# Moving the sums of the ffn's weight product, and writing out GpSimd's order around sixteen gathers, in a fused attention and ffn block

## The chip, the cores and the metric

One Trainium2 chip, one of its cores. The time is that of the device in microseconds. TensorE is called PE here, VectorE DVE, ScalarE ACT, GpSimd POOL and SyncE SP; SP only issues DMAs. PE's weight loads are listed apart as PEld.

## The reference

32 sequences of 64 tokens, 1024 wide, all in float32. A layer with a low-rank adapter per sequence, grouped-query attention with rotary embedding, then two layers with routed low-rank experts, two residuals:

```python
def cond(x, label):          # adapter chosen by the sequence's label
    low = einsum('bsi,bir->bsr', x, lora_A[label])
    return x @ W.T + einsum('bsr,or->bso', low, lora_B) * 0.5
def attn(x):                 # 32 heads of 32, 8 kv heads, causal
    q, k, v = split(x @ w_qkv.T + b_qkv)
    p = softmax(mask(rope(q) @ rope(k).T / sqrt(32)))
    return (p @ v) @ w_o.T + b_o
def cond2(x, language):      # top 2 of 8 experts of rank 16, biased by language
    gates = top2_softmax(x @ Wr.T + 5 * onehot(language))
    return x @ W2.T + 2 * einsum('bter,bte,eor->bto', x @ A, gates, B)
def ffn(x):                  # the same form, own router, with a bias
    return x @ W_base.T + b_base + 2 * experts(x)
x = x + attn(cond(x, label))
x = x + ffn(cond2(x, language))
```

## The kernel before

Two neighbouring linear layers are multiplied together first: cond's weights with w_qkv ("cq" and "ckv"), and cond2's with the ffn's base weights ("cf", with the identity added for the residual). Then two halves of 16 sequences (`hf` = 0, 1) run one after the other: projection to q and k (`qk_pair`, column groups 4, 0, 1, 2, 3), v, attention in eight units, the output projection, and the ffn.

Every large product follows one scheme: a 2 x 2 block product with seven block multiplications instead of eight (`Group`). Its steps p1, p6, p5, p7, p2, p3, p4 are each one block multiplication into the PSUM banks x, y and z; the sums of weight blocks (s1 to s4) are made on POOL (`weight_sums`, L179 to L182), those of column blocks (t1 to t4) on DVE (`column_sums`, L191 to L197). p1's result is copied by ACT (L282), p6's and p7's are added to it by DVE (`u1`, L288, and `u2`, L300), and `out` finishes a block (outputs of cq, ckv and cf: L580, L582).

**The product cf** (168 to 296 us) has four groups g = 0 to 3. Its blocks stay in SBUF, in the tile `cf`, which groups 0 and 1 fill (kappa = 0) and groups 2 and 3 fill again (kappa = 1). The ffn uses the scheme twice, one inside the other, so for each kappa seven sets of eight factors are needed: `level_one` (L741) adds whole blocks, two tiles of 128x512, `level_two` (L753 to L756) adds quarters of them and issues four DMAs of 256 KB into the scratch `cf7` (L758). All these sums are on DVE. `levels(kappa)` lists the eleven steps. The list of kappa 0 is worked off behind the steps of group 2, that of kappa 1 after the last group and after the two `low_rows` of b2f (L515). The steps also hold `narrow` (cx, a narrow product per group) and `wo_sums` (sums of w_o's blocks, one at a time: load by SP, four sums on POOL, DMA out by POOL).

Temporary tiles come from one ring of eleven, `tp`, through `tmp`: a twelfth request waits until the first tile has been read for the last time, by a DMA too. The weights `w` and the sums `s` come from rings of two.

**The ffn** runs the seven products n = 0 to 6, which are p1, p6, p2, p7, p5, p3 and p4 of the outer scheme (`SEVEN`), each in two quarters q = 0, 1; a `Quarter` is itself a group of seven blocks, 128x256 each. `begin` does p1 and p6, then the quarter before is finished (p4, p3), then `middle` does p5, p2, p7 and out11. Outer products that must be added to each other are kept in four accumulators a, b, c, z of SBUF; `known` (L1410) adds an accumulator to p1's, p6's or p7's sum on POOL, and `out_f` (L1419, L1426) adds that to the bank on DVE. `c` has the tag of `a`.

**The gathers.** The adapter's rows of each sequence are fetched by an indirect DMA, issued by POOL (L440). Those of the first half go into tiles of the pool `gen`; those of the second half into the unused half of its tile `q`, and are issued in two runs of eight, after the last POOL sum of n = 2 and of n = 3 (`late["gather0"]`, `late["gather1"]`).

**Order.** Where `tc.manual_schedule` stands, the engines named keep the order in which the code records their instructions; elsewhere a scheduler orders them by its own estimates, and it also merges what is recorded inside and outside such a block. Up to the first half's beginning SP, PE and DVE are in written order, POOL and ACT are not; in the ffn only PE is.

Of the kernel before, what the change touches and what calls it, by code (L numbers as in the profile page):

```python
# [19 lines left out]
P = 128  # L20
# [56 lines left out]
def block_kernel(ctx: ExitStack, tc: tile.TileContext, a, out: bass.AP):  # L77
# [354 lines left out]

    def gathered(hf, s, new, n):

        tiles = []
        for b0 in range(0, BS, n):
            t = new(f"a1_{hf}_{s}_{b0}")
            for b in range(n):
                at = hf * BH + s * BS + b0 + b
                nc.gpsimd.indirect_dma_start(  # L440
                    t[:, b, :],
                    None,
                    a["a1"],
                    bass.IndirectOffsetOnAxis(ap=rows_of[:, at : at + 1], axis=0),
                )
            tiles.append(t)
        return tiles
# [59 lines left out]
    with tc.tile_pool(name="gen", bufs=1) as gen:  # L507

        def low_rows(name, low, right, n, dst):

            for at in range(0, n, 512):
                m = min(512, n - at)
                ps = ps_tile(f"{name}_{at}")
                for kc in range(KC):
                    nc.tensor.matmul(  # L515
                        ps[:, :m], low[:, kc, :], right[:, kc, at : at + m],
                        start=kc == 0, stop=kc == KC - 1,
                    )
                rows = tmp(f"{name}o_{at}")
                nc.scalar.copy(rows[:, :m], ps[:, :m])  # L520
                nc.scalar.dma_start(dst[:, at : at + m], rows[:, :m])
# [112 lines left out]
        def gather_first(s):  # L634
            tags = iter(("w_os", "s_os"))
            first_pass[s] = gathered(
                0, s, lambda name: gen.tile([P, 4, KC * LR], F32, tag=next(tags), name=name), 4
            )
# [95 lines left out]
        def level_one(kappa, j, x, y, op):  # L734
            if kappa == 1 and j == 1:

                wide = gen.tile([P, H, 512], F32, tag="sum0", name="cfs1")
                spare.extend(wide[:, i, :] for i in range(4))
            s = [spare.pop() if spare else tmp(f"cfs{kappa}{j}{i}") for i in range(2)]
            for i in range(2):  # L740
                op(s[i], x[i], y[i])  # L741
            sums_of_cf[j] = s

        spare = []

# [16 lines left out]

        def levels(kappa):

            s = sums_of_cf
            v = nc.vector
            one, two = partial(level_one, kappa), partial(level_two, kappa)
            b11, b12, b21, b22 = (block_of(x) for x in ("11", "12", "21", "22"))
            return [
                lambda: one(1, b21, b22, v.tensor_add),  # L770
                lambda: two("22", b22),
                lambda: two("s1", s[1]),
                lambda: one(2, s[1], b11, v.tensor_sub),
                lambda: two("s2", s[2]),
                lambda: one(3, b11, b21, v.tensor_sub),
                lambda: two("11", b11),
                lambda: one(4, b12, s[2], v.tensor_sub),
                lambda: two("12", b12),
                lambda: two("s3", s[3]),
                lambda: two("s4", s[4]),  # L780
            ]

        steps = levels(0)

        def next_steps(n, *more):
            def do(w):
                for _ in range(n):
                    steps.pop(0)()
                for step in more:
                    step(w)  # L790

            return do

        def first_w(w):
            narrow(2, w)
            first_pass["w"] = load_w(cqkv[:, :, 4 * WG : 5 * WG], "qk04")

# [8 lines left out]
                (1, "p7"): lambda w: wo_sums(4),  # L806
                (1, "p4"): lambda w: (narrow(1, w), wo_sums(5)),
                (2, "p1"): next_steps(2),
                (2, "p6"): next_steps(2, lambda w: wo_sums(6)),
                (2, "p7"): next_steps(1),  # L810
                (2, "out11"): next_steps(2),
                (2, "p2"): next_steps(2),
                (2, "p3"): next_steps(1, lambda w: wo_sums(7)),
                (2, "p4"): next_steps(1, first_w),
                (3, "p4"): lambda w: narrow(3, w),
            },
        )
        for half in range(2):
            at = slice(half * 512, (half + 1) * 512)
            low_rows(f"b2f{half}", b2, w3[:, :, at], 512, b2s[:, at])  # L820
        for step in levels(1):
            step()

# [80 lines left out]
    def scoped(name, bufs=1, side="left"):  # L904
        return pools.enter_context(tc.tile_pool(name=name, bufs=bufs, side=side, reuse_waits="tile"))

    for hf in range(2):
        x = first_pass["x"] if hf == 0 else load_x(hf)
# [4 lines left out]

        pools = ExitStack()
        qp = scoped(f"q{hf}")
        act = scoped(f"act{hf}")
        ep = scoped(f"e{hf}", 8)
        attention, pools = pools, ExitStack()
        xt = all_column_sums(f"x{hf}", scoped(f"sums_x{hf}"), x_half, 512)
        q = qp.tile([P, 2, BH, 4, S], F32, tag="q", name=f"q_{hf}")  # L920
        if hf == 0:
            low = first_pass["low"]
        else:

            low = new_low(hf)
            a1 = q[:, 1].rearrange("p b m t -> p b (m t)")
            tiles = []
            for s in range(NS):
                with tc.issue_after(late[f"gather{s}"].ins):
                    tiles += gathered(hf, s, lambda name: a1[:, s * BS : (s + 1) * BS], BS)  # L930
            steps = [ranks(hf, s, x, tiles[s : s + 1], low) for s in range(NS)]
            first_halves, second_halves, sums = zip(*steps)
# [29 lines left out]
        def qk_pair(g, z_bank=group_bank):  # L962
            w = first_pass.pop("w", None)
            if w is None:
                w = load_w(cqkv[:, :, g * WG : (g + 1) * WG], f"qk{hf}{g}")

            def out(r, c, ps, add):
                oc = 2 * g + r
                raw = tmp(f"raw_{hf}_{oc}_{c}")
                bias = bqk[:, oc : oc + 1]  # L970
                if add is None:
                    nc.scalar.activation(raw, ps, AF.Identity, bias=bias)
                else:
                    nc.vector.scalar_tensor_tensor(raw, ps, bias, add, ALU.add, ALU.add)
                rope(oc, c, raw)

            def rank(r, c, rows):
                b = b1d[rows, g, :] if (r, c) == (0, 1) else b1q[rows, (2 * g + r) * P : (2 * g + r + 1) * P]
                return b, low_half(c)[rows]

            return RankGroup(f"qk{hf}{g}", w, weight_sums(w, f"qk{hf}{g}"), xt, out, rank, z_bank)
# [310 lines left out]

# [88 lines left out]
        def accumulator(x):  # L1384
            pool, tag = {"a": (yp, "sum3"), "b": (fp, "b"), "c": (yp, "sum3"), "z": (yp, "sum2")}[x]
            acc[x] = pool.tile([P, 4, 512], F32, tag=tag, name=f"{x}_f{hf}")

        def quarter(n, q):
# [18 lines left out]
            def known(m, half, add):  # L1407
                if prior is not None:
                    to = part(prior if kept is None else kept, m, half)
                    late["sum"] = nc.gpsimd.tensor_add(to, part(prior, m, half), add)  # L1410

            def out_f(m, half, ps, add):
# [8 lines left out]
                oc = 4 * r + q + 2 * m  # L1421
                both = m in outs
                if not both:
                    outs[m] = tmp(f"o_{hf}_{oc}_{c}")
                o = outs[m][:, half * 256 : (half + 1) * 256]
# [37 lines left out]

        with tc.manual_schedule(engines={mybir.EngineType.PE}):
            rs = [logit_rows(c) for c in range(2)]
# [16 lines left out]
            for n in range(7):  # L1482
# [3 lines left out]
                if n == 4:  # L1486

                    for kc in range(H):
                        t = by_sequence(xt.whole[1][:, kc, :])
                        nc.vector.tensor_sub(t, x_half(H + kc, 0), t)  # L1490
                for q in range(2):
                    if (n, q) == (3, 0):
                        late["gather0"] = late["sum"]
                    if (n, q) == (5, 0):
                        late["gather1"] = late["sum"]
                    group = quarter(n, q)
                    group.begin()
                    if last is not None:
                        finish(last)
                    group.middle()  # L1500
                    if q == 0 and n < 6:
                        ts[n + 1] = inner_columns(n + 1)
                    last = group
                    if (n, q) == (0, 0):
                        ps = ps_tile(f"lgx_{hf}")
# [9 lines left out]
                        for c in range(2):  # L1515
                            ps = ps_tile(f"hx_{hf}_{c}")
                            nc.tensor.matmul(ps, b2f[:, D : D + P], hw[0][c], start=True, stop=True)
                            nc.vector.tensor_add(h[1, c], h[1, c], ps)
                    if (n, q) == (1, 0):
                        gs = gates_turned("3", hf, gates3)  # L1520
# [91 lines left out]
```

## Time and profile before

Three runs: median 1222.45 us (1222.40 to 1223.41). The profiled execution took 1222.28 us, its span is 1220.5 us, granted clock 0.99 in the mean.

| stretch, us | what | PE busy | DVE | POOL | granted clock |
|---|---|---|---|---|---|
| 0 to 168 | products cq, ckv | 165.0 | 48.7 | 64.2 | 1.00 |
| 168 to 296.3 | product cf, b2f | 127.5 | 56.8 | 55.7 | 1.00 |
| 296.3 to 308.3 | first step of the first half | 3.6 | 7.9 | 0.0 | 0.79 |
| 308.3 to 604 | first half to the output projection | 295.7 | 203.9 | 154.2 | 0.99 |
| 604 to 758 | first half's ffn | 149.7 | 82.9 | 52.0 | |
| 758 to 762.2 | its last quarter | 0.0 | 0.5 | 4.2 | 0.82 |
| 762.2 to 1068 | second half to the output projection | 305.8 | 207.1 | 165.7 | 0.99 |
| 1068 to 1220.5 | second half's ffn | 147.8 | 83.6 | 36.0 | 1.00 |

Busy time is the time in which an engine runs instructions. The granted clock is the share of PE's full rate that the chip allowed in the stretch; where it is below 1, the same matmuls take longer and still count as busy. The profile's list of waits names for each engine what it waited for, the total, the number and the longest; a releaser behind an arrow is the last to come. In timeline rows an idle time in brackets is the engine's idle time just before the row.

### The profile page before, as it was taken

Reading aid. Unit: us, or ns where it says so; the run is one execution under the profiler, and the core shown is the slowest. Engines: PE = TensorE matmul, PEld = TensorE weight load, DVE = VectorE, ACT = ScalarE, POOL = GpSimd, SP = SyncE. Lnnn points to the kernel's source line nnn. Section 1 sums busy time; section 2 is a strip of 40 time slices with the busy share of each in tenths; the row PEclk is TensorE's granted clock in tenths of the full one; section 3 lists DMA queues with packets and bytes.
Section 4 is the critical chain, followed back from the end, with each engine's and each line's share of the span. In section 5 each row is a group of like instructions: output and inputs, shape, how many; then the busy total and the mean of one; then the engine's idle time right before and its main releaser. Section 6 shows DMA issues by size and latency. Waiting matters only on the chain.

```text
span 1220.5 us, 15162 instructions
## 1 busy us (share of the span) xinstructions
PE 1195.1 (98%) x5916; PEld 708.7 (58%) x5916; DVE 691.4 (57%) x1221; ACT 156.7 (13%) x302; POOL 531.9 (44%) x477
## 2 busy tenths in 40 slices
PE   9999999998899999999999898999999999999998
PEld 3444874554344468544458787544458654448887
DVE  4312151455655888774757362456788864657562
ACT  1001000000000114430011000100113431011000
POOL 3441365331143656662802453334655761822231
PEclk9999999999899999999999899999999999999999
DMA  6652734675511120222216565121120122204543
GB/s 242 224 204 107 270 130 143 217 257 172 165 35 35 35 70 2 70 70 86 86 44 190 160 186 177 53 65 39 35 69 2 71 69 70 92 26 119 156 137 105
DMA packets 114679, 136.71 MB, mean 112 GB/s; under 512 B 6576, under 2 KB 92976, under 8 KB 113328
## 3 DMA queue, kind: packets, MB, share of 16 engines
q1 hardware_dynamic: 101120, 111.52, 28.7%
q10 hardware_dynamic: 10800, 15.84, 3.7%
q0 software_dynamic: 2688, 8.39, 2.0%
q8 instruction: 47, 0.77, 0.3%
q14 instruction: 24, 0.20, 0.0%
HBM read 101.02 MB, written 34.71 MB: 111 GB/s over the span
## 4 chain that ended last, share of the span: by engine, by line
PE 94%; DMA 2%; POOL 1%; DVE 1%; issue 1%; SPq 0%; ACT 0%; DVEq 0%; ACTq 0%; POOLq 0%
PE qk_y L261 9%; PE o_y L261 7%; PE qk_z L261 6%; PE qk_x L261 6%; PE f_y L261 5%; PE v L1002 5%; PE o_x L261 5%; PE o_z L261 5%; PE f_z L261 4%; PE f_x L261 4%; PE cf_y L261 3%; PE cq_y L261 3%; PE sc L1023 3%; PE pt L1076 2%; PE cq_z L261 2%; PE cf_x L261 2%
## 5 line engine op out<-in xcount | busy, mean ns | idle before, releaser
L950 POOL TENSOR_TENSOR raw<-raw,consts 128x512 f32<-128x512 f32 x40 | 63.1, 1584 | 131.4 <-DVE t L949 131.4
L1056 POOL TENSOR_TENSOR e<-e,top 128x512 f32<-128x512 f32 x64 | 64.9, 1044 | 57.3 <-DVE top L1055 42.2
L261 PE MATMUL qk_x<-x,w_qk 128*128 128x512 f32 x160 | 75.1, 612 | 8.4 <-ACT qk_p L282 8.4
L261 PE MATMUL f_y<-s_f,w_f 128*128 128x256 f32 x336 | 82.3, 380 | 0.5 <-DVE f_u L300 0.5
L1068 POOL TENSOR_TENSOR e<-e,tot 128x512 f32<-128x512 f32 x64 | 66.2, 1065 | 27.3 <-DVE tot L1066 27.3
L261 PE MATMUL qk_y<-sum_x,s_qk 128*128 128x512 f32 x160 | 72.2, 594 | 0.0
L261 PEld LDWEIGHTS f_y<-s_f,w_f 128*128 128x128 f32 x336 | 63.9, 191 | 9.7 <-DVE f_u L300 0.9
L261 PEld LDWEIGHTS qk_x<-x,w_qk 128*128 128x128 f32 x160 | 30.9, 195 | 48.3 <-issue 39.0
L261 PE MATMUL o_x<-q,w_o 128*128 128x512 f32 x128 | 58.9, 592 | 0.0
L1002 PE MATMUL v<-w_v,x 128*128 128x256 f32 x256 | 58.7, 382 | 0.0
L1177 POOL TENSOR_TENSOR x<-x,o_u 128x512 f32<-128x512 f32 x24 | 30.9, 1292 | 54.3 <-DVE o_u L1175 33.2
L1002 PEld LDWEIGHTS v<-w_v,x 128*128 128x128 f32 x256 | 47.4, 190 | 8.4 <-issue 2.7
L261 PEld LDWEIGHTS qk_y<-sum_x,s_qk 128*128 128x128 f32 x160 | 30.3, 191 | 37.6 <-issue 36.4
L951 DVE TENSOR_TENSOR t<-t,consts 128x512 f32<-128x512 f32 x40 | 48.6, 1227 | 0.7
L1065 DVE TENSOR_REDUCE tot<-e 128x8 f32<-128x512 f32 x64 | 40.5, 666 | 10.6 <-ACT e L1060 10.4
L1060 ACT ACTIVATE e<-e 128x512 f32<-128x512 f32 x64 | 38.2, 639 | 54.2 <-POOL e L1056 54.2
L1046 DVE TENSOR_TENSOR e<-sc,consts 128x512 f32<-128x512 f32 x64 | 39.7, 675 | 8.8 <-PE sc L1023 8.8
L960 DVE TENSOR_TENSOR q<-raw,t 128x512 f32<-128x512 f32 x32 | 38.4, 1204 | 2.5 <-POOL raw L950 2.3
L1055 DVE TENSOR_REDUCE top<-e 128x8 f32<-128x512 f32 x64 | 39.5, 672 | 0.0
L261 PEld LDWEIGHTS o_x<-q,w_o 128*128 128x128 f32 x128 | 23.7, 190 | 26.8 <-issue 26.8
L1078 ACT COPY ws<-pt 128x512 f32<-128x512 f32 x64 | 33.0, 611 | 41.8 <-PE pt L1076 41.8
L261 PE MATMUL qk_y<-sum_x,w_qk 128*128 128x512 f32 x80 | 37.0, 605 | 0.0
(365 smaller groups left out, 2379.1 us busy)
## 6 DMA issues: line engine op xcount, KB each, us to landing
w_f<-cf SPq DMA_DIRECT2D x28, 512.0 KB, 4.8
w_f<-cf SPq DMA_DIRECT2D x28, 384.0 KB, 4.3
w_qk<-cqkv SPq DMA_DIRECT2D x10, 1024.0 KB, 5.6
x<-in_xT SPq DMA_DIRECT2D x16, 512.0 KB, 8.1
w_o<-in_wo SPq DMA_DIRECT2D x16, 512.0 KB, 5.1
s_o<-wos SPq DMA_DIRECT2D x16, 512.0 KB, 6.3
outT<-o ACTq DMA_DIRECT2D x32, 256.0 KB, 4.1
cqkv<-cq ACTq DMA_DIRECT2D x16, 256.0 KB, 5.3
```

Of the source, the lines that this page charges most:

```text
L261: nc.tensor.matmul(ps, self.weights[left][:, kc, :], self.right(right, kc), start=first and kc == 0, stop=kc == self.h - 1, skip_group_che ...
L950: nc.gpsimd.tensor_mul(rv, rv, c3)
L951: nc.vector.tensor_mul(t2v, t2v, s3)
L960: nc.vector.tensor_add(*unfinished.pop())
L1002: nc.tensor.matmul(begun[t], x[kc][:, t * P : (t + 1) * P], wv[:, kc, :], start=False, stop=kc == KC - 1, skip_group_check=True,)
L1023: nc.tensor.matmul(sc[j][:, n * S : (n + 1) * S], q[rows, g, b, 2 * mp : 2 * mp + 2, :].rearrange("p m t -> p (m t)"), k[rows, g, b, :], s ...
L1046: nc.vector.tensor_add(per_key(e), per_key(sc[j]), mask.unsqueeze(1).to_broadcast([P, 8, S]))
L1055: nc.vector.tensor_reduce(top, ev, AX.X, ALU.max)
L1056: nc.gpsimd.tensor_sub(ev, ev, wide(top))
L1060: nc.scalar.activation(e, e, AF.Exp, scale=SCALE)
L1065: nc.vector.tensor_reduce(tot[:, i], es[i], AX.X, ALU.add)
L1068: nc.gpsimd.tensor_mul(es[i], es[i], wide(tot[:, i]))
```

## The change

- **cf's sums.** `levels(kappa, step)` is called by name behind out11, p2, p3 and p4, for kappa 0 in group 1, for kappa 1 in group 3. Their order is another one (22; 11; s3, s1; s2, s4, 12), and all `level_one` tiles come from `tmp`. `wo_sums(5)` to `(7)` stand behind p6, p7 and p3 of group 2.
- **Rows of b2f** get a tile of their own, with the tag of the narrow weights `w3x`, instead of two `tmp` tiles.
- **The load of group 0's qk weights** of the first half is issued at the end of this part, by name (`first_pass["w0"]`).
- **The second half's tile `q`** is allocated before the first half's ffn. Its sixteen gathers are issued in the quarters of the ffn, behind `begin`: none in n = 0, two per quarter in n = 1, 2, 3, the last four in n = 4.
- **POOL's order** in the ffn is the written one, beside PE's.
- **`c` is `a`'s tile**, not a new one of its tag. **Outputs of the quarters q = 1** use one pair tile with the tag "gates" in place of two `tmp` tiles.

```diff
-    def gathered(hf, s, new, n):
+    def gather(to, at):
+        nc.gpsimd.indirect_dma_start(
+            to, None, a["a1"], bass.IndirectOffsetOnAxis(ap=rows_of[:, at : at + 1], axis=0)
+        )
+
+    def gathered(s, new, n):
...
-                rows = tmp(f"{name}o_{at}")
+                rows = tmp(f"{name}o_{at}") if rows is None else rows
...
-            if kappa == 1 and j == 1:
-
-                wide = gen.tile([P, H, 512], F32, tag="sum0", name="cfs1")
-                spare.extend(wide[:, i, :] for i in range(4))
-            s = [spare.pop() if spare else tmp(f"cfs{kappa}{j}{i}") for i in range(2)]
+            s = [tmp(f"cfs{kappa}{j}{i}") for i in range(2)]
...
-        def levels(kappa):
+        def levels(kappa, step):
...
+            if step == "out11":
+                two("22", b22)
+            elif step == "p2":
+                two("11", b11)
+            elif step == "p3":
+                one(3, b11, b21, v.tensor_sub)
+                two("s3", s[3])
+                one(1, b21, b22, v.tensor_add)
+                two("s1", s[1])
+            else:
+                one(2, s[1], b11, v.tensor_sub)
+                two("s2", s[2])
+                one(4, b12, s[2], v.tensor_sub)
+                two("s4", s[4])
+                two("12", b12)
...
-            first_pass["w"] = load_w(cqkv[:, :, 4 * WG : 5 * WG], "qk04")
+            first_pass["w4"] = load_w(cqkv[:, :, 4 * WG : 5 * WG], "qk04")
...
-                (1, "p4"): lambda w: (narrow(1, w), wo_sums(5)),
-                (2, "p1"): next_steps(2),
-                (2, "p6"): next_steps(2, lambda w: wo_sums(6)),
-                (2, "p7"): next_steps(1),
-                (2, "out11"): next_steps(2),
-                (2, "p2"): next_steps(2),
-                (2, "p3"): next_steps(1, lambda w: wo_sums(7)),
-                (2, "p4"): next_steps(1, first_w),
-                (3, "p4"): lambda w: narrow(3, w),
+                (1, "out11"): lambda w: levels(0, "out11"),
+                (1, "p2"): lambda w: levels(0, "p2"),
+                (1, "p3"): lambda w: levels(0, "p3"),
+                (1, "p4"): lambda w: (levels(0, "p4"), narrow(1, w)),
+                (2, "p6"): lambda w: wo_sums(5),
+                (2, "p7"): lambda w: wo_sums(6),
+                (2, "p3"): lambda w: wo_sums(7),
+                (2, "p4"): first_w,
+                (3, "out11"): lambda w: levels(1, "out11"),
+                (3, "p2"): lambda w: levels(1, "p2"),
+                (3, "p3"): lambda w: levels(1, "p3"),
+                (3, "p4"): lambda w: (levels(1, "p4"), narrow(3, w)),
...
+        b2f_rows = gen.tile([P, 2, 512], F32, tag="w3x", name="b2f_rows")
         for half in range(2):
...
-            low_rows(f"b2f{half}", b2, w3[:, :, at], 512, b2s[:, at])
-        for step in levels(1):
-            step()
+            low_rows(f"b2f{half}", b2, w3[:, :, at], 512, b2s[:, at], b2f_rows[:, half])
+        first_pass["w0"] = load_w(cqkv[:, :, :WG], "qk00")
...
-            for s in range(NS):
-                with tc.issue_after(late[f"gather{s}"].ins):
-                    tiles += gathered(hf, s, lambda name: a1[:, s * BS : (s + 1) * BS], BS)
+            tiles = [a1[:, s * BS : (s + 1) * BS] for s in range(NS)]
...
-            w = first_pass.pop("w", None)
+            w = first_pass.pop(f"w{g}", None)
...
+        gathers = []
+        if hf == 0:
+            ffn_pools, pools = pools, ExitStack()
+            next_q = new_q(1)
+            next_pools, pools = pools, ffn_pools
+            for b in range(BH):
+                gathers.append(partial(gather, next_q[:, 1, b].rearrange("p m t -> p (m t)"), BH + b))
...
-            pool, tag = {"a": (yp, "sum3"), "b": (fp, "b"), "c": (yp, "sum3"), "z": (yp, "sum2")}[x]
-            acc[x] = pool.tile([P, 4, 512], F32, tag=tag, name=f"{x}_f{hf}")
+            pool, tag = {"a": (yp, "sum3"), "b": (fp, "b"), "z": (yp, "sum2"), "c": (None, None)}[x]
+            acc[x] = acc["a"] if x == "c" else pool.tile([P, 4, 512], F32, tag=tag, name=f"{x}_f{hf}")
...
+                if not outs and q:
+                    outs["pair"] = fp.tile([P, 2, 512], F32, tag="gates", name=f"o_{hf}_{step}")
                 if not both:
-                    outs[m] = tmp(f"o_{hf}_{oc}_{c}")
+                    outs[m] = outs["pair"][:, m] if q else tmp(f"o_{hf}_{oc}_{c}")
...
-        with tc.manual_schedule(engines={mybir.EngineType.PE}):
+        with tc.manual_schedule(engines={mybir.EngineType.PE, mybir.EngineType.Pool}):
...
-                for q in range(2):
-                    if (n, q) == (3, 0):
-                        late["gather0"] = late["sum"]
-                    if (n, q) == (5, 0):
-                        late["gather1"] = late["sum"]
-                    group = quarter(n, q)
+                for r in range(2):
+                    group = quarter(n, r)
                     group.begin()
+                    for _ in range((0, 2, 2, 2, 5, 3, 2)[n]):
+                        if gathers:
+                            gathers.pop(0)()
```

More of the change, by code (lines that the diff above doesn't have):

```diff
@@ L431, in block_kernel @@
     hp = ctx.enter_context(tc.tile_pool(name="hp", bufs=2))
-    def gathered(hf, s, new, n):
+    def gather(to, at):
[3 more added lines that the diff above has]
+    def gathered(s, new, n):
         tiles = []
         for b0 in range(0, BS, n):
-            t = new(f"a1_{hf}_{s}_{b0}")
+            t = new(f"a1_0_{s}_{b0}")
             for b in range(n):
[L439 to L445, printed above, removed]
+                gather(t[:, b, :], s * BS + b0 + b)
             tiles.append(t)
@@ L507, in block_kernel, with low_rows @@
     with tc.tile_pool(name="gen", bufs=1) as gen:
-        def low_rows(name, low, right, n, dst):
+        def low_rows(name, low, right, n, dst, rows=None):
             for at in range(0, n, 512):
@@ L636, in gather_first @@
             first_pass[s] = gathered(
-                0, s, lambda name: gen.tile([P, 4, KC * LR], F32, tag=next(tags), name=name), 4
+                s, lambda name: gen.tile([P, 4, KC * LR], F32, tag=next(tags), name=name), 4
             )
@@ L742, in level_one @@
             sums_of_cf[j] = s
-        spare = []
         def level_two(kappa, left, x):
@@ L768, in levels @@
             b11, b12, b21, b22 = (block_of(x) for x in ("11", "12", "21", "22"))
[L769 to L792, printed above, removed]
+            if step == "out11":
[13 more added lines that the diff above has]
+                two("12", b12)
         def first_w(w):
             narrow(2, w)
-            first_pass["w"] = load_w(cqkv[:, :, 4 * WG : 5 * WG], "qk04")
+            first_pass["w4"] = load_w(cqkv[:, :, 4 * WG : 5 * WG], "qk04")
         multiply(
@@ L905, in scoped, with new_q @@
         return pools.enter_context(tc.tile_pool(name=name, bufs=bufs, side=side, reuse_waits="tile"))
+    def new_q(hf):
+        return scoped(f"q{hf}").tile([P, 2, BH, 4, S], F32, tag="q", name=f"q_{hf}")
     for hf in range(2):
@@ L912, in x_half @@
             return x[kc].rearrange("p (b c t) -> p b c t", c=2, t=S)[:, :, c, :]
-        pools = ExitStack()
-        qp = scoped(f"q{hf}")
+        if hf == 0:
+            pools = ExitStack()
+            q = new_q(0)
+        else:
+            pools, q = next_pools, next_q
         act = scoped(f"act{hf}")
@@ L919, in block_kernel @@
         xt = all_column_sums(f"x{hf}", scoped(f"sums_x{hf}"), x_half, 512)
-        q = qp.tile([P, 2, BH, 4, S], F32, tag="q", name=f"q_{hf}")
         if hf == 0:
@@ L926, in block_kernel @@
             a1 = q[:, 1].rearrange("p b m t -> p b (m t)")
-            tiles = []
-            for s in range(NS):
-                with tc.issue_after(late[f"gather{s}"].ins):
-                    tiles += gathered(hf, s, lambda name: a1[:, s * BS : (s + 1) * BS], BS)
+            tiles = [a1[:, s * BS : (s + 1) * BS] for s in range(NS)]
             steps = [ranks(hf, s, x, tiles[s : s + 1], low) for s in range(NS)]
@@ L1291, in block_kernel @@
             attention.close()
+        gathers = []
+        if hf == 0:
+            ffn_pools, pools = pools, ExitStack()
[3 more added lines that the diff above has]
+                gathers.append(partial(gather, next_q[:, 1, b].rearrange("p m t -> p (m t)"), BH + b))
         late["pool"] = fp = scoped(f"ffn{hf}", side="right")
@@ L1409, in known @@
                     to = part(prior if kept is None else kept, m, half)
-                    late["sum"] = nc.gpsimd.tensor_add(to, part(prior, m, half), add)
+                    nc.gpsimd.tensor_add(to, part(prior, m, half), add)
             def out_f(m, half, ps, add):
@@ L1500, in block_kernel @@
                     group.middle()
-                    if q == 0 and n < 6:
+                    if r == 0 and n < 6:
                         ts[n + 1] = inner_columns(n + 1)
                     last = group
-                    if (n, q) == (0, 0):
+                    if (n, r) == (0, 0):
                         ps = ps_tile(f"lgx_{hf}")
@@ L1518, in block_kernel @@
                             nc.vector.tensor_add(h[1, c], h[1, c], ps)
-                    if (n, q) == (1, 0):
+                    if (n, r) == (1, 0):
                         gs = gates_turned("3", hf, gates3)
```

## The prediction

> **What bounds the kernel.** I read in this order: busy time by engine, PE's own waits, the granted clock around each wait, then the timeline at each place.
>
> ```profile
> PE 1195.1 (98%) x5916; PEld 708.7 (58%) x5916; DVE 691.4 (57%) x1221; ACT 156.7 (13%) x302; POOL 531.9 (44%) x477
> ...
> PE qk_x L261 <- ACT qk_p L282: 8.4, 1, 8.4
> PE f_z L261 <- DVE o L1426: 4.3, 1, 4.3
> PE f_z L261 <- DVE c_f L1419: 4.2, 1, 4.2
> PE idle L134 <- DVE idle L131: 1.5, 1, 1.5
> PE cq_z L261 <- DVE cq L582: 0.8, 1, 0.8
> ```
>
> PE computes for all but 25.4 us of 1220.5, and the change removes no matmul, so it can only win idle time and what follows it. Three waits matter; start and tail (the rest) are not touched. The stretches around the first wait, and one with a short wait:
>
> ```profile
> 308.30:313.70 5.40, 5.40 (x7) 2.30 (x8) 5.40 (x10) 0.00 (x0) 0.00 (x0) 0.51 1.03 340
> 313.70:320.00 6.30, 6.30 (x16) 2.72 (x15) 2.65 (x5) 0.00 (x0) 0.00 (x0) 1.00 0.61 165
> ...
> 40.00:50.00 10.00, 9.22 (x22) 3.91 (x21) 1.98 (x3) 0.00 (x0) 3.30 (x4) 1.00 0.66 205
> ```
>
> The third number from the end is the granted clock: 0.51 for 5.4 us after the wait, then 1.00; after an idle of 0.78 us (the last line) it stays 1.00. A long wait is so paid twice. From the chain of waits:
> - **Wait 1** (299.9 to 308.3): 8.40, then 6 passes of qk_x in 5.45 where 8 take 3.43 (2.57 for 6): 2.87 more. Together 11.3.
> - **Wait 2** (689.5 to 693.8): 4.24; then f_z x8 in 3.78 for 1.73, f_x in 1.71 for 0.86, f_y 0.92 for 0.86: 2.96. Together 7.2.
> - **Wait 3** (758.0 to 762.2): 4.28; then f_z 2.07 and 1.71 for 0.86 each, 102 h in 2.32 for 1.54 (at the 1.93 per 128 of the next h row): 2.84. Together 7.1.
>
> What released each:
>
> ```profile
> 307.65 0.59 ACT L282 COPY qk_p<-qk_x 128x512 f32<-128x512 f32 x1 [10.57 <-DMA cf<-cft]
> ...
> 690.23 0.95 POOL L440 DMA_INDIRECT q<-in_a,rows_of  x1 [0.30 <-issue]
> 691.20 1.41 POOL L1410 TENSOR_TENSOR c_f<-b_f,f_p 128x256 f32<-128x256 f32 x2
> ...
> 757.28 1.26 POOL L179 TENSOR_TENSOR s_qk<-w_qk 128x512 f32<-128x512 f32 x1 [7.89 <-DMA w_qk<-cqkv]
> ...
> 760.94 0.72 POOL L1410 TENSOR_TENSOR c_f<-c_f,f_u 128x256 f32<-128x256 f32 x1
> ```
>
> Wait 1 is the ring of 11 tmp tiles: qk_p gets one only when a write of the cf sums lands. Wait 2 is eight gathers standing on GpSimd ahead of a sum that PE's bank needs. Wait 3 is three s_qk sums, waiting for a weight load, ahead of the last such sum.
>
> **Part by part.**
>
> *The sums of cf* (levels). The same sums and 56 writes of 256 KB, at other places: kappa 0 behind group 1's steps, kappa 1 behind group 3's. Before, all of kappa 1 stood at the end, DVE from 279.7 on, with idles of 5.73 and 3.87 behind the DMAs of b2f0o and b2f1o. b2f gets tiles of its own, so those idles go (DVE, beside PE work: no gain by themselves). Afterwards, in group 3: the sum behind p3 ends at 276.3 (before: 275.62+0.69); two first levels (1.28 each) and two second levels (four 128x256 of 0.42, overlapping: 1.5) make 5.6, to 281.9; p4's output 0.7; then 2 x 1.28 + 3 x 1.5 = 7.1, to 289.7. Beside GpSimd's s_qk sums (270 to 275) a DVE sum is slower (L753 took 1.50 instead of 0.42 beside s_cf at 234.8), so up to 291.5. sum_x (4 x 2.49) follows; its t2, which p6 needs, is there by 296.5, before b2f ends at 299.7. The 11th tmp tile before qk_p is one of the first of p4's sums, written out by about 294. **Wait 1 as such goes: 11.3.**
>
> What is late next: the load of w_qk00. It now stands last on SP, behind these writes. In the built order of the changed kernel one matmul of group 0 (qk_z from the first s_qk sum of w_qk00) stands directly behind pair 4's p1, ahead of everything else; before, nothing of group 0 stood there. So PE at 299.7 waits for that load and one GpSimd sum. The last 20 writes start when the first s3 tile is ready, 278.3 to 280.1. SP's own rate, 302 to 313 us before, is 0.75 us a write at 340 GB/s and a DMA share of 1.03. That gives 293.3 to 295.1 for w_qk00. Such a load lands after 5.2, median 5.6, at most 6.8; with the queue full 299 to 302; L179 1.26: 300.2 to 303.2. **New wait 0.5 to 3.5; I take 2.3**, past the middle because the rows of b2f (256 KB each) share the queues.
>
> Does this short wait halve the clock too? The nearest rows, 4.24 and 4.28, both did; 0.78 did not. [...] By the row the place costs 2.3 + 2.9[...], and keep 2.9 for the range. **Net of this part: 11.3 - 2.3 = 9.0.**
>
> Kappa 0 now falls behind group 1: 5.6 + 0.7 + 7.1 of DVE from 220.8, to about 234.5, before group 2's u1, which p7 needs at 237.4. p1's copy waits for a tmp tile whose write issues near 231 and lands by 235 (3.3 median): u1 ends near 236.4. Cost nothing, with 1 us of cover; if the writes lag, 0 to 1.5. Group 3's w load slips from 227.3 to some 238 behind them, lands by 245; PE wants it at 254.8, and its s2 (GpSimd to 250) at 258.3: nothing. The last three wo sums follow on SP and GpSimd; before, the last ended at 267.6, now about 270, and w_qk04's sums near 275 where PE wants them at 299.9: nothing.
>
> *The gathers*. 16 of 0.95 to 1.33 with 0.30 between. Now two per quarter in n = 1 to 3, then four. In the built order each pair stands between a sum from p6 (u1) and the one from p7 (u2). From p6's end: DVE 0.43 and sum 0.72, so gathers from 1.2 to 3.7 (4.5 at the slowest). PE does five blocks of 0.86 to p7's end at 4.3, u2 is there at 4.8. Cover 0.3 to 1.1, and 0.85 more before p3 wants the bank. The four in n = 4, 5.0 us, stand where p5 has no such sum. SP is not involved, 2 MB of DMA are only spread. h, near 755, finds all landed. **Gain 7.2**, bounds 5 to 7.2.
>
> *Written order on GpSimd in the ffn*. It would suggest that wait 3 goes as well. But s_qk of the second half is recorded outside this block, and in the built order three of its sums still stand before the last a_f sum, as before. The load issues when PE releases the ring (750.3), unchanged. **Gain 0**, bounds 0 and 7.1.
>
> *c in a's tile; o tiles of q = 1 in "gates"; q allocated earlier*. The outs take six tmp tiles less per half. The gates tile is free once turned (PE gpr, about 655), before the first pair (680). A pair waits for the last pair's writes, 16 us older, landing 4.1. The end (last o at 1216.3, then one 256 KB write) is the same. Nothing, -0.3 to +0.5.
>
> **Sum.** Against the execution's own 1222.28 (1220.5 of span and 1.8 around it): 9.0 + 7.2 = 16.2, so 1206.1; the median of the runs is 0.17 higher: **1206.2**.
>
> **Rivals.**
> - *Two waits go, a short one comes* (0.55): 1204.3 to 1208 by the bounds above, 1206.2.
> - *The load comes in time* (0.12): the wait at 299.7 under 0.5. For it: SP issues a free write in 0.36 to 0.5. Against: the stretch of 302 to 313 us, where SP had nothing to wait for, moved no more than 340 GB/s. 1222.45 - 18.5 = 1204.0.
> - *The load comes later [...]* (0.18), because GpSimd slows DVE more or the queue is fuller: 4 + 2.9 = 6.9 at this place, 1210.9.
> - *Wait 3 goes too* (0.06): 1206.2 - 7.1 = 1199.1. For it only that the runtime order of SP or DMA makes the load early; the order of the sums speaks against it.
> - *Only one of the two goes, or a new wait in groups 2 and 3* (0.06): 1212 to 1219.
> - *Slower* (0.03): gathers stretch. [...] they now stand among DVE's work in every quarter. A pair has 3.6 + 0.85 = 4.45 us. From 2.2 us a gather PE waits, and over six quarters all 16.2 are lost at 2.2 + 16.2/12 = 3.6. At 4 us: 1206.2 + 6 x 3.55 = 1227.5. Against it: the slowest of 16 took 1.33, with DVE busy beside.
>
> Faster by over 0.2% (2.4 us, about what a measurement can tell) 0.96, within 0.01, slower 0.03. The range 1202.5 to 1212 leaves out wait 3's case, the slower one and most of the "only one" case, and is above all the late load's spread.
>
> **What would show it.** PE's waits: no qk_x <- ACT qk_p of 8 us; instead qk_z <- POOL s_qk of 0.5 to 3.5 near 300. No f_z <- DVE after n = 3. f_z <- DVE o of 4.3 still there, near 742 now, with the clock at half behind it. Gathers 0.95 to 1.33 from 650 on. DVE at sum_x by 292. The prediction is wrong if that last wait is gone, if the clock is at half after 300, or if cf_y waits in group 2.

## The result, and the profile after

| | median, us | runs | of the kernel before, same chip |
|---|---|---|---|
| changed kernel | 1213.33 | 1211.33 to 1214.05 | 1222.74; ratio 0.992 (0.9903 to 0.9937) |
| changed kernel, second set | 1211.82 | 1211.02 to 1212.10 | 1222.81; ratio 0.9913 (0.9896 to 0.9929) |

The change brought 9.4 and 11.0 us, not the 16.2 that were predicted. The profiled execution took 1214.05 us, its span is 1212.3 us: it is the slowest of its four.

The row of busy times and PE's list of waits, of the changed kernel (line, tile, what it waited for: total, times, longest):

```profile
PE 1191.3 (98%) x5916; PEld 705.9 (58%) x5916; DVE 701.6 (58%) x1221; ACT 156.6 (13%) x302; POOL 533.7 (44%) x477
...
PE qk_z L261 <- POOL s_qk L179: 6.8, 1, 6.8
PE f_z L261 <- DVE o_p L1425: 4.0, 1, 4.0
PE cf_x L261 <- ACT cf_p L282: 1.6, 1, 1.6
```

Two of the old waits are gone, ACT's qk_p and the first f_z. The last f_z is still there. In place of the first stands a wait for POOL's s_qk, at the predicted place and with the predicted releaser, but of 6.8 us, not 2.3. The stretches around it (engines with busy time, then from the right GB/s, DMA share, granted clock):

```profile
296.00:302.00 6.00, 5.97 (x14) 2.28 (x12) 6.00 (x11) 0.59 (x1) 0.00 (x0) 1.00 1.04 348
302.00:308.70 6.70, 0.00 (x0) 0.00 (x0) 3.43 (x6) 0.59 (x1) 1.25 (x2) 0.90 0.71 223
308.70:314.00 5.30, 5.24 (x6) 2.19 (x7) 0.00 (x0) 0.00 (x0) 3.71 (x4) 0.50 0.11 6
```

PE does nothing for 6.7 us, and then runs at clock 0.50 for 5.3. Six records behind the wait (qk_z x2, qk_x x4) took 5.29 us, where they take 2.66 at full clock (the first profile of the run e1 below, 300.27 to 302.93): 2.6 us more. The place costs 6.8 + 2.6 = 9.4. Before, counted in the same way from start to start, it was 8.40 + 2.7 = 11.1 (six passes from 308.29 to 313.57, for 2.57).

The timeline shows how the wait came about (start, duration, engine, line, operation, in brackets the idle time before it):

```profile
274.75 4.35 DVE L749 TENSOR_TENSOR cft<-cf,cft 128x256 f32<-128x256 f32 x1
275.10 1.28 POOL L179 TENSOR_TENSOR s_qk<-w_qk 128x512 f32<-128x512 f32 x1
276.32 1.27 POOL L181 TENSOR_TENSOR s_qk<-w_qk 128x512 f32<-128x512 f32 x1
277.54 1.26 POOL L180 TENSOR_TENSOR s_qk<-s_qk,w_qk 128x512 f32<-128x512 f32 x1
278.88 1.34 POOL L182 TENSOR_TENSOR s_qk<-w_qk,s_qk 128x512 f32<-128x512 f32 x1
...
300.25 1.20 SPq L425 DMA_DIRECT2D w_qk<-cqkv  x1
302.01 0.59 ACT L282 COPY qk_p<-qk_x 128x512 f32<-128x512 f32 x1 [2.85 <-PE qk_x L261]
307.45 1.26 POOL L179 TENSOR_TENSOR s_qk<-w_qk 128x512 f32<-128x512 f32 x1 [27.23 <-DMA w_qk<-cqkv]
308.76 1.22 PE L261 MATMUL qk_z<-sum_x,s_qk 128*128 128x512 f32 x1 [6.79 <-POOL s_qk L179]
```

A sum of 0.42 us on DVE lasted 4.35 while POOL made its sums of w_qk04. All that DVE does for kappa 1 slid back with it, and SP's writes, and at their end the load of w_qk00: issued at 300.25 (predicted 293.3 to 295.1), landed 7.2 us later. ACT's copy had no tmp tile to wait for: wait 1 as such is gone.

Where the 8.2 us of the two spans lie (before and after, starts of the same instruction): qk_x of pair 4 at 296.3 and 298.4 (+2.1; of this 1.6 is the wait for ACT's cf_p in the list above, at 174 us), that pair's next step at 313.57 and 314.05 (+0.5), the first h of the second half at 755.38 and 748.13 (-7.3), its qk_x at 768.26 and 759.80 (-8.5).

### The profile page after: what moved, and what is told of

Same layout as the page of the kernel before. It is cut to its first block, busy times and chain, and to the rows that moved or that the text cites. A ratio compares the mean times of both kernels' runs of the same rounds, so it can differ in the third digit from the quotient of the medians.

```text
span 1212.3 us, 15157 instructions
## 1 busy us (share of the span) xinstructions
PE 1191.3 (98%) x5916; PEld 705.9 (58%) x5916; DVE 701.6 (58%) x1221; ACT 156.6 (13%) x302; POOL 533.7 (44%) x477
## 4 chain that ended last, share of the span: by engine, by line
PE 92%; DVE 4%; DMA 2%; issue 1%; POOL 0%; SPq 0%; DVEq 0%; POOLq 0%
PE qk_y L261 9%; PE o_y L261 7%; PE f_y L261 6%; PE qk_z L261 6%; PE qk_x L261 6%; PE v L990 5%; PE o_x L261 5%; PE o_z L261 5%; PE f_z L261 4%; PE f_x L261 4%; PE cq_y L261 3%; PE cf_y L261 3%; PE sc L1011 3%; PE pt L1064 2%; PE cq_z L261 2%; PE f_z L273 2%
## 5 line engine op out<-in xcount | busy, mean ns | idle before, releaser
L261 PE MATMUL qk_z<-sum_x,s_qk 128*128 128x512 f32 x80 | 37.4, 608 | 6.8 <-POOL s_qk L179 6.8
L948 DVE TENSOR_TENSOR q<-raw,t 128x512 f32<-128x512 f32 x32 | 38.4, 1205 | 2.5 <-POOL raw L938 2.3
L179 POOL TENSOR_TENSOR s_qk<-w_qk 128x512 f32<-128x512 f32 x10 | 19.8, 1976 | 42.9 <-DMA w_qk<-cqkv 42.9
```

The lines of the kernel that those rows point to most:

```text
L261: nc.tensor.matmul(ps, self.weights[left][:, kc, :], self.right(right, kc), start=first and kc == 0, stop=kc == self.h - 1, skip_group_che ...
L948: nc.vector.tensor_add(*unfinished.pop())
```

## Experiments

The theory: the new wait needs the load of w_qk00 at the end of SP's queue and the one early matmul of group 0 behind p1; it grew because POOL's s_qk sums of w_qk04 held DVE back. Rivals: sum_x on DVE would stop PE there anyway; the tmp tiles are still short; the writes alone set the time of the load.

### The load ahead of the last twelve writes (e1)

```diff
+        def load_w0():
+            first_pass["w0"] = load_w(cqkv[:, :, :WG], "qk00")
...
-                (3, "p4"): lambda w: (levels(1, "p4"), narrow(3, w)),
+                (3, "p4"): lambda w: (narrow(3, w), load_w0(), levels(1, "p4")),
...
-        first_pass["w0"] = load_w(cqkv[:, :, :WG], "qk00")
```

> Only the load of w_qk00 moves, on SP's queue: ahead of the last 12 writes of kappa 1's sums instead of behind all of them. The built order of PE, GpSimd and VectorE is that of the changed kernel. Theory A (the place of this load is what the wait at 302 is made of): the load issues near 289 and lands by 297, the wait of 6.8 us for GpSimd's s_qk and the half clock behind it (2.9) both go, 1213.3 - 9.7 = 1203.6; 1203 to 1205. Rival B (VectorE's sums are late enough to stop PE there by themselves): the wait changes its releaser to sum_x on VectorE and keeps 2 to 5 us, 1206 to 1210. Rival C (the tmp tiles are still short): a wait for ACT's qk_p comes back, since the last writes land 1 us later, 1208 to 1213.

Four runs gave 1202.37, 1212.00, 1202.14 and 1210.47 (median 1206.42, ratio 0.9886, 0.9845 to 0.9928): two times, the lower a little below theory A's 1203 to 1205, the upper that of rivals B or C. One more execution of the same kernel followed.

> A second look at the kernel with w_qk00's load ahead of the last 12 writes, which gave two times each near 1202.3 and near 1211. Its first profile fell on 1202.4. There GpSimd's s_qk sums of w_qk00 ran at 295.8 to 300 beside VectorE's second sum_x sum (5.70 us in place of 2.49). Theory: in the executions of 1211 a GpSimd sum comes a little earlier or later and holds VectorE back by more than the 0.5 us that was left before PE wants that sum, which is then a wait of 3 us or more and a half clock of 2 to 3 us near 300. If this execution is one of 1202, nothing is decided. Rival: the 8 to 9 us lie elsewhere in the kernel.

It took 1210.08. Timeline of the first execution (1202.37), rows of DVE and POOL:

```profile
295.76 1.27 POOL L179 TENSOR_TENSOR s_qk<-w_qk 128x512 f32<-128x512 f32 x1 [17.24 <-DMA w_qk<-cqkv]
296.99 1.71 POOL L181 TENSOR_TENSOR s_qk<-w_qk 128x512 f32<-128x512 f32 x1
297.50 5.70 DVE L193 TENSOR_TENSOR sum_x<-x,sum_x 128x512 f32<-128x512 f32 x4
```

And of the second (1210.08):

```profile
296.39 8.74 POOL L179 TENSOR_TENSOR s_qk<-w_qk 128x512 f32<-128x512 f32 x1 [17.92 <-DMA w_qk<-cqkv]
296.71 2.49 DVE L193 TENSOR_TENSOR sum_x<-x,sum_x 128x512 f32<-128x512 f32 x4
299.12 2.49 DVE L195 TENSOR_TENSOR sum_x<-x,x 128x512 f32<-128x512 f32 x4
301.53 2.49 DVE L197 TENSOR_TENSOR sum_x<-x,sum_x 128x512 f32<-128x512 f32 x4
...
305.19 2.08 PE L261 MATMUL qk_z<-sum_x,s_qk 128*128 128x512 f32 x2 [4.32 <-POOL s_qk L179]
```

The load came at 296 in both, in time. In the first, POOL's sums got through and DVE's four took 5.70 instead of 2.49: nobody wants those so soon, and PE's list has no wait there. In the second, DVE got through with twelve sums in a row, POOL's one sum took 8.74 instead of 1.27, and PE waited 4.32 for it with a half clock behind. With the load in time the old wait goes, so its place is part of what that wait was made of; but a wait of another make can take its place, and my guess of who suffers was the wrong way round, since it was POOL that was held. Rivals B and C fall: the releaser is neither sum_x nor qk_p. That the other three executions follow the same two patterns is inferred from their times alone.

### w_qk04's sums earlier (e3)

```diff
-                (2, "p3"): lambda w: wo_sums(7),
-                (2, "p4"): first_w,
+                (2, "p4"): lambda w: (first_w(w), wo_sums(7)),
```

> The load of w_qk04 and GpSimd's s_qk sums of it come ahead of the last wo sum instead of behind it; w_qk00 stays last on SP. Theory D (the new wait grew from the 2.3 us that I predicted to 6.8 because these s_qk sums ran at 275 to 280, beside kappa 1's first sums, and held VectorE back by 4.1 us): the sums run near 268 to 273, the cft sum of 4.35 us takes 0.4 to 1.5, the 20 last writes and w_qk00 come 3 to 4 us earlier, the wait at 302 shrinks to 2.5 to 4; [...] the clock stays at 1.00: 1213.3 - 4 - 2.9 = 1206.4; if the clock is halved nevertheless, 1209.3. Rival E (the writes set the time of the load by themselves, not VectorE): the wait stays at 6 to 7 us and the time at 1212 to 1214.

1208.24 (1207.33 to 1209.63), ratio to before 0.9888 (0.9871 to 0.9905). Timeline:

```profile
266.77 1.26 POOL L182 TENSOR_TENSOR s_qk<-w_qk,s_qk 128x512 f32<-128x512 f32 x1
...
272.14 0.42 DVE L749 TENSOR_TENSOR cft<-cf,cft 128x256 f32<-128x256 f32 x1
...
294.69 0.69 SPq L425 DMA_DIRECT2D w_qk<-cqkv  x1
...
302.84 1.70 PE L261 MATMUL qk_z<-sum_x,s_qk 128*128 128x512 f32 x2 [2.88 <-POOL s_qk L179]
```

POOL is done with w_qk04 at 268, the DVE sum takes 0.42, the load issues at 294.69, inside what I had predicted for the change itself, and the wait is 2.88. Theory D holds and rival E falls. But the clock:

```profile
299.84:303.25 3.41, 0.53 (x2) 0.30 (x2) 0.00 (x0) 0.59 (x1) 1.72 (x2) 1.00 0.50 175
303.25:306.66 3.41, 3.41 (x5) 1.35 (x4) 0.00 (x0) 0.00 (x0) 3.24 (x3) 0.50 0.15 8
306.66:310.07 3.41, 3.41 (x9) 1.52 (x8) 0.00 (x0) 0.00 (x0) 0.00 (x0) 1.00 0.00 0
```

It was 0.50 for 3.41 us (third number from the end): behind this wait of 2.88 it was halved too, but for a shorter time than the 6.83 us behind the wait of 6.79. The six records took 4.37 (302.84 to 307.21) in place of 2.66, so 1.7 are lost. Of the two values expected, 1206.4 and 1209.3, the result lies between, nearer to the halved one.

### The early matmul in its group (e9)

```diff
+        with tc.manual_schedule(engines={mybir.EngineType.PE}) if hf == 0 else ExitStack():
             pair.main(1 + hf)
             for g in (0, 1):
...
             pair.last_rows()
             pair.out01()
```

(p1 of the first half stands in such a block too.)

> PE's order is written out from pair 4 through groups 0 and 1 of the first half: the one matmul of group 0 (qk_z from w_qk00's first sum) that stood directly behind pair 4's p1 now stands in group 0, and so do three other pieces of order among pair 4's own steps. The load stays last on SP. Theory A': the wait needs both the late load and that one matmul; with it in its group, w_qk00 is wanted 20 us later than it lands, the wait and the half clock go, 1203 to 1206. Rival B as in the run before: sum_x takes over, 1206 to 1210. Rival F: pair 4's own sums (s_qk of w_qk04) or the load lateness act elsewhere, PE waits 6 to 7 us inside group 0: 1211 to 1214.

1203.04 (1201.96 to 1204.18), ratio 0.9847 (0.983 to 0.9864). The load still issued late, at 298.00, and no wait is left near 300. The wait needs both: a late load, and a matmul that asks for it 20 us ahead of its group. (The edit writes out PE's whole order there, so three other pieces of pair 4's order moved as well; none of them had a wait in the changed kernel.) Against the repeated 1211.82 the gain is 8.8, by the two ratios 8.1; the place's cost in that execution is 8.8 (6.24 of wait and 2.6 of half clock).

### The two halves of the change (e6, e7)

e6 is the kernel before with the ffn's part alone, e7 the kernel before with the cf part alone.

> The kernel before with only the ffn's part of the change (gathers between GpSimd's sums in the written order, c in a's tile, the o tiles of their own); the cf sums stay as they were. Theory: wait 2 alone goes, 4.2 plus the half clock behind it, 1222.7 - 7.2 = 1215.5; wait 3 keeps its 4.0 but its half clock covers some 1 us less, 1214.5. Wait 1 is back, 8.4 for ACT's qk_p. Rival: the written order itself gives or costs something in the ffn, then the result lies outside 1213.5 to 1216.5.

> The kernel before with only the cf part of the change (levels behind each block, kappa 0 and 1 apart, b2f in tiles of its own); the ffn as before. Theory: wait 1 turns into the wait for w_qk00 of about 6.8 and its half clock, so this part brings 1 to 3 us by itself: 1219.5 to 1221.5; with the 1215.5 of the ffn's part alone the two add up to the change, 1222.3 - 6.8 - 2 = 1213.5. Rival: the parts need each other (the cf part has its wait only beside the ffn's order), then 1212 or 1222.5 and over.

e6: 1215.51 (1214.93 to 1217.45), ratio 0.9952 (0.9934 to 0.9969), with 8.4 for qk_p and one f_z of 4.0. e7: 1220.47 (median of 20), ratio 0.9982 (0.9976 to 0.9989), with 6.3 for s_qk and both f_z waits. So 6.8 and 1.9 us, together 8.8, against 9.4 and 11.0 of the whole. The parts are near enough independent; the 0.6 to 2.2 left over are of the size by which the runs of one kernel differ, and aren't attributed.

### The last sum ahead of s_qk (e4)

```diff
-                    nc.gpsimd.tensor_add(to, part(prior, m, half), add)
+                    late["sum"] = nc.gpsimd.tensor_add(to, part(prior, m, half), add)
...
-        pair = qk_pair(4)
         if hf == 0:
+            pair = qk_pair(4)
             pair.p1()
         else:
+            with tc.issue_after(late["sum"].ins):
+                pair = qk_pair(4)
```

> The changed kernel with GpSimd's last a_f sum of the ffn's first half written ahead of the four s_qk sums of the second half's first weights; nothing else moves. Theory: wait 3 (4.02 near 751, and the half clock behind it, 2.1 to 2.8) is made of the three s_qk sums that stand ahead of that sum and wait for their load: 1213.0 - 6.1 = 1206.9. Rival: the o tiles or the outs set that wait, it keeps 3 us or more: 1212 to 1214. Against the theory would also be a new wait for s_qk in the second half's first block, where PE wants it.

1208.37 (1207.60 to 1209.44), 1.5 above the expectation. Wait 3 is gone, without a new wait for s_qk, so the theory holds. But PE stood still at a place where it had not before, in the h matmuls a few us later:

```profile
756.76 1.21 PE L458 MATMUL h<-x,q 128*32 128x64 f32 x71
759.58 1.00 PE L458 MATMUL h<-x,q 128*32 128x64 f32 x57 [1.61 <-issue]
```

"issue" means that it waited for nothing that the profile shows.

### The three orders together, and six more matmuls (e11, e12)

> The changed kernel with three pieces of order mended: PE's one early matmul of group 0 in its group (as in e9), w_qk04's load and sums ahead of the last wo sum (as in e3), the last a_f sum ahead of s_qk (as in e4). Theory: e9's 1203.0 less wait 3's 6.0, and VectorE 4 us earlier, which nothing waits for: 1197.0; 1196 to 1198.5. Rival: the waits are followed by others that they hid: 1199 to 1203.

1198.79 (1198.16 to 1199.67), ratio 0.9806 (0.9786 to 0.9827): faster than both kernels, and 0.3 above the range expected. The same gap, at the same count of records:

```profile
745.54 1.21 PE L458 MATMUL h<-x,q 128*32 128x64 f32 x71
...
748.63 1.79 PE L458 MATMUL h<-x,q 128*32 128x64 f32 x57 [1.89 <-issue]
```

e12 is e11 with this edit:

```diff
-    for n in (512, 512, 128):
+    for n in (512, 512, 128) + 6 * (64,):
```

> The three mended orders of e11 and six more matmuls of 128x64 on zeros at PE's start, whose results nobody reads. In e11 and in e4 PE stood still for 1.89 and 1.61 us inside the h matmuls of the second half, behind the same 71 of 128 records, with no semaphore to wait for, and one packet of the instruction queue moved in that microsecond. Theory G (PE has run ahead of the loading of its instructions, and the place is fixed in the instruction stream): each matmul has two records, so 12 more records come ahead and the gap stands behind 59, not 71; the time is e11's plus 0.5 to 1. Rival (another engine or a bank ends it): the gap stays behind 71.

```profile
746.08 1.08 PE L458 MATMUL h<-x,q 128*32 128x64 f32 x59
749.35 1.20 PE L458 MATMUL h<-x,q 128*32 128x64 f32 x69 [2.18 <-issue]
```

Behind 59, as theory G says: 12 records more moved it by 12. The gap belongs to a place in PE's instruction stream, not to a semaphore. Just ahead of each gap the trace has one packet of the instruction queue; this is its row in the DMA view of e12 for 746.8 to 747.0 us (packets, MB, share of the time):

```profile
q8 instruction: 1, 0.02, 33.6%
```

The gap ends 2.3 to 2.5 us after the packet's begin in all three (e4: 757.3 and 759.58; e11: 746.1 and 748.63; e12: 746.9 and 749.35). The packet after it comes 3.4 to 3.7 us later. In e9 the packet came at 750.3, and PE reached the same place only at about 752.7: no gap.

e12 took 1197.47 (1196.67 to 1198.95), ratio 0.9794 (0.9778 to 0.981), not more than e11 as expected: behind its gap the clock stayed at 1.00, behind that of e11 it fell to 0.50 for 3.4 us. In the changed kernel wait 3, 4.02 us, stands just ahead of this place, and PE has no gap there; with wait 3 gone e4 has one of 1.61. So only part of what wait 3 cost was had by order alone. That its 4 us gave the loading of the instructions time to run ahead would be theory G's reading; no trace shows the loading's lead.

### The changed kernel again

> The changed kernel once more, for the spread of its time (1211.3 to 1214.1) and of its two new waits: 6.79 for s_qk of w_qk00 and 1.60 for ACT's cf_p. Theory: the first stands in every execution at 6 to 7 us with a half clock behind it; the second comes and goes with the landing of group 0's w_cf load, and with it 1 to 2 us of the time: 1211.5 to 1214. Rival: both belong to the change, and both are there again at the same size.

1211.82; wait for s_qk 6.24, none for cf_p. qk_x of pair 4 begins at 296.44, as before the change, not at 298.38. The wait of 1.60 and the 2.1 us that it goes with are not in every execution.

## Why the prediction was wrong

- **Wait 1 goes as such: right.** qk_p had its tile at once.
- **The new wait: right in mechanism and place, wrong in size.** I named w_qk00's load, last on SP behind the writes, and the one early matmul. "New wait 0.5 to 3.5; I take 2.3" measured 6.79 and 6.24. The step that failed stands ahead of it, the price of GpSimd's sums on VectorE: "Beside GpSimd's s_qk sums a DVE sum is slower (L753 took 1.50 instead of 0.42 ...), so up to 291.5". I let the slowdown cost 1.8 at most; it was 4.35 - 0.42 = 3.9 at one sum and 1.1 at the next (L584, 1.35 for 0.28). The row that I took, 1.50, was a sum that met one POOL sum. Here four stood in a row: the sum of 4.35 us ended at 279.10, behind the third (278.80), and the next one at 280.37, behind the fourth (280.22). The lost 5.0 are close to the length of the whole run (1.28 + 1.27 + 1.26 + 1.34 = 5.1). The profile before could have told: behind the row that I took stand two more, each beside a POOL sum of its own (L180, 236.00 to 237.44, and L182, 237.51 to 238.84), 3.1 lost in all.

```profile
234.81 1.50 DVE L753 TENSOR_TENSOR cft0s<-cfs,cfs 128x256 f32<-128x256 f32 x1
236.35 1.37 DVE L754 TENSOR_TENSOR cft0s<-cft0s,cfs 128x256 f32<-128x256 f32 x1
237.64 1.48 DVE L755 TENSOR_TENSOR cft0s<-cfs 128x256 f32<-128x256 f32 x1
```

e3 takes this term away, and the wait becomes 2.88. VectorE, which I had at sum_x "by 292", came there at 295.7 (293.5 in the repeated profile, without the early shift). The rest of the sum was right: behind the last sum of p3 (282.5 in the profile after) the levels took 5.6 and 7.1 us to the tenth, and a write 0.78 for 0.75. Issued last, the load landed after 6.8 to 7.2 (the changed kernel twice, e3, e9), where I had "at most 6.8".
- **The clock: wrong.** I put the half clock at 0 for a wait of 2.3; that was an estimate, for which the profile before has, after PE's start, no wait between 0.78 and 4.24. At 6.79 us the clock was halved as behind the rows of 4.24 and 4.28, so 2.6 of the miss followed from the first error; but e3 shows that the choice itself was wrong: at 2.88 the clock was halved and cost 1.7, between the 0 and the 2.9 that I kept for the range. The sign that I had named for being wrong, half clock after 300, came.
- **The rival of the later load** had this case at 0.18, with 4 + 2.9 at 1210.9. It was the right one; measured 6.8 + 2.6. Of its two reasons the first holds ("GpSimd slows DVE more"); the fuller queue added at most 0.4 to the landing.
- **Wait 2: right.** 7.2 predicted; the way from 314 to 748 us became 7.7 shorter, e6 brought 6.8. (My sums of all three waits took the rows' durations, whose ends reach into the next row; from start to start they come to 11.1, 7.0 and 7.0, not 11.3, 7.2 and 7.1.) The gathers took 0.95 to 1.28 and nothing waited: the rival of stretched gathers did not come about at two in a row.
- **Wait 3 stays: right**, 4.02 for 4.28; the half clock behind it cost 1.8 for 2.84, about 1 us that I had not counted: it lasted 3.41 us in place of 6.83, which I take for luck of the moment (see the last section). e4 shows that its cause is the one given.
- **Kappa 0 in group 2: right.** No wait of PE there.

In the profile's own numbers: 16.2 predicted, less 7.4 at the new wait (9.0 forecast; from +2.1 to +0.5 it was 1.6), less 2.1 of the execution's early shift, plus 0.5 at wait 2 and 1.2 at and behind wait 3, less 0.2 in the rest, is 8.2.

## What to carry to other kernels

When work is moved on VectorE, look for what GpSimd does at that time, and count a whole run of sums on the other engine as the price (here 5.0 us lost beside 5.1 of GpSimd's sums), not one row in which they happened to meet for a moment. Before a load is put at the end of a queue, look in the built order for the first matmul that asks for it, which may stand far ahead of its group; writing that order out brought 8 to 9 us in all four runs here, where the load's own place brought as much in only two of five. And when a wait is removed, ask what had gone on behind it: with wait 3 gone (e4), PE stood still at the next place, and the gain was 3.5 to 5.0 us (against the two sets) where the wait and its half clock had cost 5.8.

## What was not expected of the hardware

- **GpSimd and VectorE held each other up for whole runs of instructions.** A VectorE sum of 0.42 us took 4.35 and ended behind the third of GpSimd's sums beside it (the changed kernel); a GpSimd sum of 1.27 took 8.74 beside twelve VectorE sums (e1, second execution). One and the same kernel took 1202 or 1211 us; in its two profiles GpSimd got through first in the faster execution and VectorE in the slower. What decides who gets through, these runs don't show.
- **The half clock did not go by the length of the wait alone.** By granted clock behind the wait: 1.60 us (the changed kernel, cf_p) and 1.61 (e4), 1.00; 1.89 (e11), 0.50; 2.18 (e12), 1.00; 2.88 (e3), 0.50; from 4.02 (the changed kernel, wait 3) to 8.40 (before, wait 1), 0.50. Up to the tail, the changes of the clock lie whole multiples of 3.413 us apart in the profiles before and after: before at 303.32, 313.56, 692.44, 699.27, 760.71 and 767.53 (3, 111, 2, 18 and 2 times), after at 307.37, 314.19, 754.51 and 757.92 (2, 129 and 1). Stretches of 3.41 us in e11, e12 and e4 (the second number is the time that PE computed in the stretch, the third from the end the clock):

```profile
745.28:748.69 3.41, 1.52 (x76) 1.10 (x79) 3.41 (x5) 1.19 (x2) 1.88 (x2) 1.00 0.15 52
748.69:752.10 3.41, 3.41 (x59) 2.32 (x60) 3.41 (x3) 0.60 (x1) 3.33 (x3) 0.50 0.02 5
...
747.92:751.33 3.41, 1.98 (x71) 1.53 (x72) 3.41 (x7) 1.19 (x2) 2.19 (x1) 1.00 0.05 10
...
756.92:760.33 3.41, 1.80 (x125) 1.64 (x120) 3.41 (x5) 1.18 (x2) 2.37 (x2) 1.00 0.07 20
```

The gap of 1.89 in e11 lay in one stretch, and the next one ran at half. The 2.18 of e12 fell on two stretches, 0.75 and 1.43, and the clock stayed; the 1.61 of e4 left 1.80 of work in its stretch, and it stayed too. The time that PE computed in a stretch doesn't settle it either: e11's 1.52 was followed by 0.50, the 1.43 of the changed kernel from 300.54 to 303.95 by 1.00 (the ends of matmuls are modelled there). At half clock, in the profiles before and after, it stayed half behind stretches with 0, 1.86, 1.88, 2.02 and 2.06 us of work, and rose behind those with 3.19 and 3.41. The half clock lasted 3.41 us in e3, 6.83 in the changed kernel and 10.24 at wait 1 before, and cost about half of what PE computed in it (1.7 of 3.41 in e3, 2.6 of 5.29 in the changed kernel). What sets it, these runs don't show.
- **PE stood still at a fixed place of its instruction stream.** In the h matmuls it takes a record every 17 ns (71 in 1.21 us), and stood for 1.6 to 2.2 us, until some 2.4 us after one packet of the instruction queue. Theory G, that it had run ahead of the loading of its instructions, fits, but no trace shows the loading's lead. The place is shown by e12; that the packet is what PE waits for is inferred from the moments, in three runs with the gap and one without.
